# The last pass's first layer in two parts of three slices instead of three parts of two

## The chip, the cores and the metric

One core of a Trainium2 chip runs the whole program. The metric is the device time of one launch in microseconds (us), median over several runs. The engines are TensorE (PE in the profile; PEld is its weight load), VectorE (DVE), ScalarE (ACT), GpSimd (POOL) and the queue engine SyncE (SP). They run side by side[...].

## The reference

The input is an image batch x of 8 x 96 x 96 positions with 192 channels, in float32. Two residual blocks are applied one after the other. What follows is the reference cut to the second block's end, which is where the change lies:

```
x = x + L0(gn(x))            # group norm, 192->384, 3x3 conv, four scans, layer norm, 384->192
y = depthwise_conv7x7(gn(x)) + dw_bias
y = (y - mean(y)) * rsqrt(var(y) + 1e-6) * ln_gamma + ln_beta     # over the 192 channels
y = y @ w0 + b0              # 192 -> 768
y = gelu(y)
y = y @ w1 + b1              # 768 -> 192
x = x + y * gamma
```

## The kernel before

The program is five passes over the batch, one after the other, with arrays in device memory between them. The first pass normalizes, turns and projects x (lines 348 to 395). The second does the 3 x 3 convolution and the scans (L579 to L649). The third does the layer norm and the projection back to 192 channels (L831 to L865). The fourth does the 7 x 7 convolution, as products with band matrices (L1009, L1024), and leaves its result in `Y_d`. The last pass, from line 1093, does the rest of the second block: layer norm, first layer, gelu, second layer, residual. The change is in the last pass alone.

The last pass works in 96 units, `u` = 0 to 95. A unit is 768 positions: four image columns (`WH = 4`) of 96 rows for two images. Channels lie on partitions for the first layer, so the 192 channels of two images, 384 values, fill three blocks of 128 partitions, `yT[:, 0..2]`. Block 0 and block 2 hold 128 channels of one image each; block 1 holds the remaining 64 channels of one image in its upper half and of the other in its lower half.

The steps of a unit, each a function in the code:

- `stats_e(u, j)` and `norm_e(u, j)`, for j = 0 to 7: mean and variance of one column (L1144, L1145 on VectorE), the power -1/2 of the variance (L28 on VectorE, L29 on GpSimd), and the normalized values `yn` (L1154 on VectorE).
- `turn_in(u, k)`, k = 0 to 2: TensorE turns one block of `yn` by four transposes (L1169) into a PSUM tile `pt`, and VectorE copies it to `yT` (L1173).
- `first_layer(u, mb)`: the 768 outputs are NE = 6 slices of 128. For each slice m and image q there is one PSUM tile `hp` of 128 x 384. It takes one product with 128 channels on the contracted side (L1186) and one with 64 (L1196); then ScalarE applies the gelu and writes `g` (L1205).
- `second_layer(u, k)`, k = 0 to 2: one block of 128 positions of both images. For each image six products, one for each slice, are summed in a PSUM tile `po` (L1216). VectorE adds the residual `r` and writes `xo` (L1223), and GpSimd issues two transfers to the output (L1234).
- `load_r(u)`, `bias_r(u)`: the residual is loaded by SyncE's queue (L1124), and GpSimd adds the second layer's bias (L1133).

Every float32 product appears in the profile as two weight loads and two matmul records, a transpose as one of each. A first-layer part of two slices is therefore 8 records of L1186 and then 8 of L1196, and one `second_layer` call is 24 records of L1216. The two 64-channel products of a slice, for q = 0 and q = 1, use different halves of the partitions, and their records come in pairs that start within 0.01 us of each other.

The order on every engine is the order in which the code issues the instructions (`tc.manual_schedule()`). In the loop over units, three units are in work at once: the first layer of u, the second layer of u - 1, the turning of u + 1, and the statistics and normalization of u + 2. PSUM has eight banks for each partition. The pools of this pass take two for `pt`, four for `hp` and two for `po`. A pool hands out its banks in turn, and the first writer of a reused bank waits until the bank's last reader has finished:

```
ps_t = ph.enter_context(tc.tile_pool(name="e_ps_t", bufs=2, space=PSUM))
ps_h = ph.enter_context(tc.tile_pool(name="e_ps_h", bufs=4, space=PSUM))
ps_o = ph.enter_context(tc.tile_pool(name="e_ps_o", bufs=2, space=PSUM))
```

Of the kernel before, what the change touches and what calls it, by code (L numbers as in the profile page):

```python
# [8 lines left out]
F32 = mybir.dt.float32  # L9
# [3 lines left out]
PSUM = bass.MemoryType.PSUM  # L13
# [71 lines left out]
def conv_blocks_kernel(  # L85
# [32 lines left out]
    B, S, _, D = x.shape  # L118
# [4 lines left out]
    NE = EXP // 128  # L123
# [97 lines left out]
    with ExitStack() as ph:  # L221
# [6 lines left out]
        ps_t = ph.enter_context(tc.tile_pool(name="a_ps_t", bufs=2, space=PSUM))  # L228
# [239 lines left out]
        with tc.manual_schedule():  # L468
# [13 lines left out]
            for b in range(B):  # L482
                more = b + 1 < B
                for t in range(n_t):
                    u = b * n_t + t
# [279 lines left out]
    with ExitStack() as ph:  # L765
# [170 lines left out]
        n_u = BP * NH * n_c  # L936
# [153 lines left out]

    WH = 4
    WE = 2 * WH
    HE = 128 // WH
    with ExitStack() as ph:
        ip = ph.enter_context(tc.tile_pool(name="e_in", bufs=2))
        sp = ph.enter_context(tc.tile_pool(name="e_small", bufs=3))
        tp = ph.enter_context(tc.tile_pool(name="e_t", bufs=2))
        ps_t = ph.enter_context(tc.tile_pool(name="e_ps_t", bufs=2, space=PSUM))  # L1100
        ps_h = ph.enter_context(tc.tile_pool(name="e_ps_h", bufs=4, space=PSUM))
        ps_o = ph.enter_context(tc.tile_pool(name="e_ps_o", bufs=2, space=PSUM))

        def place(n):
            bp, n = divmod(n, PH * NV)
            return (bp, *divmod(n, NV))

        per = WQ // WH
        n_y = BP * PH * NV
        n_u = n_y * per  # L1110
        ys, rs_, mvs, rss, yns, yTs, gs, xos = {}, {}, {}, {}, {}, {}, {}, {}

        def load_y(n):
            bp, p, a = place(n)
            ys[n] = ip.tile([S, D, 2 * WQ], F32, tag="y", name=f"y_{n}")
            nc.sync.dma_start(ys[n], Y_d[PH - 1 - p :: PH, bp, a])

        def load_r(u):
            n, t = divmod(u, per)
            bp, p, a = place(n)  # L1120
            v = a * WQ + t * WH
            rs_[u] = ip.tile([128, S // HE, 2 * D], F32, tag="r", name="r", bufs=4)
            for k in range(S // HE):
                nc.sync.dma_start(  # L1124
                    rs_[u][:, k],
                    X2_d[bp, p, k * HE : (k + 1) * HE, v : v + WH].rearrange(
                        "h v b c -> h v (b c)"
                    ),
                )

        def bias_r(u):
            r = rs_[u].rearrange("p k (b c) -> p (k b) c", b=2)
            nc.gpsimd.tensor_tensor(  # L1133
                r, r, b1g.unsqueeze(1).to_broadcast([128, 2 * S // HE, D]), ALU.add
            )

        def stats_e(u, j):
            n, t = divmod(u, per)
            if j == 0:
                if t == 0 and n + 1 < n_y:  # L1140
                    load_y(n + 1)
                mvs[u] = sp.tile([S, WE, 2], F32, tag="mv", name="mv")
            st = sp.tile([S, 6], F32, tag="st", name="st", bufs=4)
            nc.vector.bn_stats(st, ys[n][:, :, t * WE + j])  # L1144
            nc.vector.bn_aggr(mvs[u][:, j], st)  # L1145
            if j == WE - 1:
                rss[u] = sp.tile([S, WE], F32, tag="rs", name="rs")
                rsqrt_eps(nc, sp, rss[u], mvs[u][:, :, 1], LN1_EPS, neg_half, "rs_ve")

        def norm_e(u, j):  # L1150
            n, t = divmod(u, per)
            if j == 0:
                yns[u] = sp.tile([S, WE, D], F32, tag="yn", name="yn", bufs=2)
            nc.vector.tensor_scalar(  # L1154
                yns[u][:, j],
                ys[n][:, :, t * WE + j],
                mvs[u][:, j, 0:1],
                rss[u][:, j : j + 1],
                ALU.subtract,
                ALU.mult,  # L1160
            )

        def turn_in(u, k):
            if k == 0:
                yTs[u] = tp.tile([128, 3, S, WH], F32, tag="yT", name="yT")
            yp = yns[u].rearrange("p (j i) c -> p j (i c)", i=2)
            pt = ps_t.tile([128, WH, S], F32, tag="pt", name="pt")
            for j in range(WH):
                nc.tensor.transpose(  # L1169
                    pt[:, j], yp[:, j, k * 128 : (k + 1) * 128], ident[:S, :S]  # L1170
                )

            nc.vector.tensor_copy(  # L1173
                yTs[u][:, k].rearrange("p h j -> p j h"), pt[:, :, ::-1]
            )

        def first_layer(u, mb):
            if mb == 0:
                gs[u] = tp.tile([128, NE, 2, WH * S], F32, tag="g", name="g")
            yT, g = yTs[u].rearrange("p k h j -> p k (h j)"), gs[u]  # L1180
            ms = (2 * mb, 2 * mb + 1)
            hps = {}
            for m in ms:
                for q in range(2):
                    hps[m, q] = ps_h.tile([128, WH * S], F32, tag="hp", name="hp")
                    nc.tensor.matmul(  # L1186
                        hps[m, q],
                        w0w[:, 2 * q, m * 128 : (m + 1) * 128],
                        yT[:, 2 * q],
                        start=True,  # L1190
                        stop=False,
                    )
            for m in ms:
                for q in range(2):
                    p = slice(q * DH, (q + 1) * DH)
                    nc.tensor.matmul(  # L1196
                        hps[m, q],
                        w0w[p, 1, m * 128 : (m + 1) * 128],
                        yT[p, 1],
                        start=False,  # L1200
                        stop=True,
                    )
            for m in ms:
                for q in range(2):
                    nc.scalar.activation(  # L1205
                        g[:, m, q], hps[m, q], AF.Gelu, bias=b0g[:, m : m + 1], scale=1.0
                    )

        def second_layer(u, k):
            if k == 0:  # L1210
                xos[u] = tp.tile([128, S // HE, 2, D], F32, tag="xo", name="xo")
            g, xo = gs[u], xos[u]
            po = ps_o.tile([128, 2, D], F32, tag="po", name="po")
            for q in range(2):
                for m in range(NE):
                    nc.tensor.matmul(  # L1216
                        po[:, q],
                        g[:, m, q, k * 128 : (k + 1) * 128],
                        w1g[:, m],
                        start=(m == 0),  # L1220
                        stop=(m == NE - 1),
                    )
            nc.vector.tensor_tensor(  # L1223
                xo[:, k].rearrange("p b c -> p (b c)"),
                po.rearrange("p b c -> p (b c)"),
                rs_[u][:, k],
                ALU.add,
            )
            n, t = divmod(u, per)
            bp, p, a = place(n)  # L1230
            w = (a * WQ + t * WH) * PH + p
            we = w + (WH - 1) * PH + 1
            for b in range(2):
                nc.gpsimd.dma_start(  # L1234
                    out[2 * bp + b, k * HE : (k + 1) * HE, w:we:PH, :], xo[:, k, b]
                )

        assert S // HE == 3
        with tc.manual_schedule():
            load_y(0)  # L1240
            load_r(0)
            for u in range(2):
                for j in range(WE):
                    stats_e(u, j)
                for j in range(WE):
                    norm_e(u, j)
                if u == 0:
                    for k in range(3):
                        turn_in(0, k)
            for u in range(n_u + 1):  # L1250
                for k in range(3):
                    if u < n_u:
                        first_layer(u, k)
                    if u + 1 < n_u:
                        turn_in(u + 1, k)
                    if k == 0:
                        if u + 1 < n_u:
                            load_r(u + 1)
                        if u < n_u:
                            bias_r(u)  # L1260
                    if u + 2 < n_u:
                        if k < 2:
                            for j in range(4 * k, 4 * k + 4):
                                stats_e(u + 2, j)
                        else:
                            for j in range(WE):
                                norm_e(u + 2, j)
                    if u >= 1:
                        second_layer(u - 1, k)


# [45 lines left out]
```

## Time and profile before

| what | value |
|---|---|
| time, three runs | 6007.35, 6009.42, 6020.1 us; median 6009.42 us |
| profiled execution | 6011.68 us; its span 6009.9 us |
| mean granted TensorE clock | 0.973 |
| PE busy | 5680.5 us, 95% of the span |
| PEld, DVE, ACT, POOL busy | 66%, 57%, 41%, 44% of the span |
| last pass on PE | from its first transpose at 3541.5 us to its last product near 5998 us |

The page gives busy shares over the whole span, but the five passes have different limits, so each pass has to be read by itself. In a group's row, the number after the last bar is the time in which the engine stood idle just before these instructions, and after the arrow stands what ended it. In the timeline, a row is a run of like instructions: its start, the time from the first one's start to the last one's end, the engine, the line, what is written and read, and how many. A matmul's modelled length is longer than its pitch, because matmuls overlap: the pitch is the distance of starts.

### The profile page before, as it was taken

How to read it: one execution, taken by the hardware profiler on the slowest of the kernel's cores; microseconds unless marked ns; L12 is line 12 of the kernel's file. 1: busy time of each engine (PE TensorE's matmuls, PEld its weight loads, DVE VectorE, ACT ScalarE, POOL GpSimd, SP SyncE). 2: the span in 40 equal slices, each digit the busy share in tenths (PEclk: the TensorE clock that was granted, in tenths of full speed). 3: DMA queues.
4: the chain of work that ended last, by engine and by line, in shares of the span. 5: the costliest groups of instructions: out<-in, count | busy, mean ns of one | idle time of the engine just before them, and what ended most of it. 6: DMA issues, size and time to landing. Idle time of an engine off the chain costs nothing.

```text
span 6009.9 us, 122810 instructions
## 1 busy us (share of the span) xinstructions
PE 5680.5 (95%) x48550; PEld 3943.4 (66%) x48550; DVE 3454.0 (57%) x8023; ACT 2440.3 (41%) x6146; POOL 2634.7 (44%) x2835
## 2 busy tenths in 40 slices
PE   6999989999998999999677769999999999999999
PEld 3655633333336989898666657777777777777777
DVE  5555469999995667777532334444444444444442
ACT  2444457777774555555333322222222222222221
POOL 1111148888886666666444422322332233233222
PEclk9999989999999999999888889999999999999999
DMA  7999779999987888888899952222222222222221
GB/s 206 282 285 258 219 213 243 244 242 244 244 231 210 266 261 268 262 267 261 232 286 290 284 141 69 66 72 63 79 64 78 64 79 64 78 64 77 61 64 37
DMA packets 570206, 1054.36 MB, mean 175 GB/s; under 512 B 109575, under 2 KB 426260, under 8 KB 567328
## 3 DMA queue, kind: packets, MB, share of 16 engines
q1 hardware_dynamic: 439344, 593.23, 37.8%
q0 software_dynamic: 124160, 450.67, 24.1%
q8 instruction: 384, 6.29, 0.5%
q10 hardware_dynamic: 6128, 2.61, 0.2%
q14 instruction: 190, 1.56, 0.1%
HBM read 585.19 MB, written 476.57 MB: 177 GB/s over the span
## 4 chain that ended last, share of the span: by engine, by line
PE 77%; DMA 6%; DVE 1%; issue 1%; SPq 1%; POOL 1%; ACT 0%; DVEq 0%; POOLq 0%; ACTq 0%
PE po L1216 19%; PE po L833 13%; PE hp L1186 12%; PE pl L579 10%; PE hp L1196 7%; PE pa L600 5%; PE pt L831 4%; DMA xin<-X_d 4%; PE py L1024 2%; PE pt L1169 2%; PE pa L603 2%; DMA Y_d<-yo 1%; DVE xin L1009 1%; DMA band<-Z_d 0%; SPq L1063 0%
## 5 line engine op out<-in xcount | busy, mean ns | idle before, releaser
L1205 ACT ACTIVATE g<-hp,b0g 128x384 f32<-128x384 f32 x1152 | 573.9, 580 | 1856.4 <-PE hp L1196 1856.4
L1216 PE MATMUL po<-w1g,g 128*128 128x192 f32 x6912 | 1178.3, 327 | 0.0
L1216 PEld LDWEIGHTS po<-w1g,g 128*128 128x128 f32 x6912 | 1116.6, 190 | 1.6 <-issue 1.1
L833 PE MATMUL po<-wc,mt 128*96 128x193 f32 x4608 | 912.8, 333 | 0.0
L1173 DVE COPY yT<-pt 128x384 f32<-128x384 f32 x288 | 251.4, 873 | 1126.7 <-PE pt L1169 1126.4
L1234 POOL DMA_DIRECT2D out_dram<-xo x576 | 321.3, 560 | 1147.9 <-DVE xo L1223 1119.4
L1186 PE MATMUL hp<-yT,w0w 128*128 128x384 f32 x2304 | 794.4, 488 | 0.4 <-ACT g L1205 0.4
L833 PEld LDWEIGHTS po<-wc,mt 128*96 128x96 f32 x4608 | 701.8, 163 | 68.6 <-ACT mean L837 65.0
L579 PE MATMUL pl<-pin,band 34*32 34x380 f32 (+1 forms) x13824 | 629.9, 489 | 19.3 <-DMA pin<-P_d 18.5
L1186 PEld LDWEIGHTS hp<-yT,w0w 128*128 128x128 f32 x2304 | 431.4, 191 | 231.6 <-issue 2.6
L609 DVE TENSOR_TENSOR_SCAN z<-decay,loc 128x768 f32<-128x768 f32 x288 | 505.9, 1756 | 61.2 <-ACT loc L588 31.7
L1024 PE MATMUL py<-xin,band 63*64 63x248 f32 (+1 forms) x6912 | 405.5, 394 | 138.3 <-DVE xin L1009 136.2
L649 POOL TENSOR_TENSOR mo<-mo,z 128x768 f32<-128x768 f32 x288 | 529.6, 1839 | 3.3 <-ACT mo L604 0.4
L618 DVE TENSOR_TENSOR_SCAN z<-decay,z 128x768 f32<-128x768 f32 x288 | 498.2, 1730 | 0.0
L579 PEld LDWEIGHTS pl<-pin,band 34*32 34x32 f32 x13824 | 232.8, 107 | 398.7 <-issue 397.1
L1024 PEld LDWEIGHTS py<-xin,band 63*64 63x64 f32 x6912 | 345.0, 142 | 198.5 <-DVE xin L1009 123.5
L840 ACT ACTIVATE sq<-pt,mean 96x384 f32<-96x384 f32 x768 | 443.0, 577 | 25.7 <-ACT mean L837 0.8
L1196 PE MATMUL hp<-yT,w0w 64*128 64x384 f32 x2304 | 449.4, 508 | 0.0
L600 PE MATMUL pa<-loc,mix 128*32 128x384 f32 x3456 | 431.9, 493 | 0.0
L603 PE MATMUL pa<-last,down 96*32 96x384 f32 x1152 | 426.9, 493 | 0.9 <-ACT mo L604 0.9
L29 POOL TENSOR_TENSOR rs<-rs_ve,neg_half 96x8 f32<-96x8 f32 x96 | 158.6, 1652 | 606.3 <-DVE rs_ve L28 606.3
L362 PE MATMUL pm<-xT,win 128*128 128x384 f32 x1152 | 395.9, 494 | 3.3 <-DVE po L386 3.3
(116 smaller groups left out, 7707.4 us busy)
## 6 DMA issues: line engine op xcount, KB each, us to landing
P_d<-po POOLq DMA_DIRECT2D x96, 1152.0 KB, 9.9
pin<-P_d SPq DMA_DIRECT2D x192, 576.0 KB
mt<-M_d SPq DMA_DIRECT2D x576, 192.0 KB
xq<-in_x_dram SPq DMA_DIRECT2D x96, 576.0 KB
xr<-in_x_dram SPq DMA_DIRECT2D x384, 144.0 KB
X_d<-x1u POOLq DMA_DIRECT2D x192, 288.0 KB, 4.2
X_d<-x1c SPq DMA_DIRECT2D x192, 288.0 KB
y<-Y_d SPq DMA_DIRECT2D x24, 2304.0 KB
```

What stands on the lines that cost most here:

```text
L579: nc.tensor.matmul(pls[g][at * RB : (at + 1) * RB, :, lo:hi], band[rows, c, kh, :], pin[rows, c, :, NJ - 1 - j, lo + kh - 1 : hi + kh - 1] ...
L600: nc.tensor.matmul(pa[at], mix[:, i, at], loc[:, q], start=True, stop=True)
L603: nc.tensor.matmul(pa[at], down[:, to], last[:, q], start=True, stop=True)
L609: nc.vector.tensor_tensor_scan(zf, decay_f, loc.rearrange("p q n -> p (q n)"), 0.0, ALU.mult, ALU.add)
L618: nc.vector.tensor_tensor_scan(zr, decay_f, zr, 0.0, ALU.mult, ALU.add)
L649: nc.gpsimd.tensor_tensor(m, m, z, ALU.add)
L833: nc.tensor.matmul(po[:S, b], lhs[m], wc[:, m], start=(m == 0), stop=(m == NC - 1))
L1024: nc.tensor.matmul(pys[t // 2][g][k * 64 : (k + 1) * 64, t % 2, :, lo:hi], pair[k][0][rows, c, d * ZS : d * ZS + 64], pair[k][1][rows, t, ...
L1186: nc.tensor.matmul(hps[m, q], w0w[:, 2 * q, m * 128 : (m + 1) * 128], yT[:, 2 * q], start=True, stop=False,)
L1196: nc.tensor.matmul(hps[m, q], w0w[p, 1, m * 128 : (m + 1) * 128], yT[p, 1], start=False, stop=True,)
L1205: nc.scalar.activation(g[:, m, q], hps[m, q], AF.Gelu, bias=b0g[:, m : m + 1], scale=1.0)
L1216: nc.tensor.matmul(po[:, q], g[:, m, q, k * 128 : (k + 1) * 128], w1g[:, m], start=(m == 0), stop=(m == NE - 1),)
```

## The change

The first layer of a unit is issued in two parts of three slices, where it was three parts of two. A part needs six `hp` tiles at once, so the PSUM pools are divided anew: one bank for `pt`, and seven in one pool that `hp` and `po` share. The loop body over k is written out, since the parts no longer go one with each k. On TensorE, a unit's order was

first layer (2 slices), turn 0, second layer 0; first layer (2), turn 1, second layer 1; first layer (2), turn 2, second layer 2

and becomes

first layer (3 slices), turn 0, second layer 0, turn 1; first layer (3), turn 2, second layer 1, second layer 2.

On VectorE the copies of turn 1 and turn 2 now follow one another, the second half of the statistics comes after both, and the normalization stands between the residual additions of second layer 1 and second layer 2. The orders on ScalarE, GpSimd and the SyncE queue stay as they were.

```diff
-        ps_t = ph.enter_context(tc.tile_pool(name="e_ps_t", bufs=2, space=PSUM))
-        ps_h = ph.enter_context(tc.tile_pool(name="e_ps_h", bufs=4, space=PSUM))
-        ps_o = ph.enter_context(tc.tile_pool(name="e_ps_o", bufs=2, space=PSUM))
+        ps_t = ph.enter_context(tc.tile_pool(name="e_ps_t", bufs=1, space=PSUM))
+        ps_h = ph.enter_context(tc.tile_pool(name="e_ps_h", bufs=7, space=PSUM))
...
-            ms = (2 * mb, 2 * mb + 1)
+            ms = range(mb * NE // 2, (mb + 1) * NE // 2)
...
-            po = ps_o.tile([128, 2, D], F32, tag="po", name="po")
+            po = ps_h.tile([128, 2, D], F32, tag="hp", name="po")
...
-                for k in range(3):
-                    if u < n_u:
-                        first_layer(u, k)
-                    if u + 1 < n_u:
-                        turn_in(u + 1, k)
-                    if k == 0:
-                        if u + 1 < n_u:
-                            load_r(u + 1)
-                        if u < n_u:
-                            bias_r(u)
-                    if u + 2 < n_u:
-                        if k < 2:
-                            for j in range(4 * k, 4 * k + 4):
-                                stats_e(u + 2, j)
-                        else:
-                            for j in range(WE):
-                                norm_e(u + 2, j)
-                    if u >= 1:
-                        second_layer(u - 1, k)
+                if u < n_u:
+                    first_layer(u, 0)
+                if u + 1 < n_u:
+                    turn_in(u + 1, 0)
+                    load_r(u + 1)
+                if u < n_u:
+                    bias_r(u)
+                if u + 2 < n_u:
+                    for j in range(4):
+                        stats_e(u + 2, j)
+                if u >= 1:
+                    second_layer(u - 1, 0)
+                if u + 1 < n_u:
+                    turn_in(u + 1, 1)
+                if u < n_u:
+                    first_layer(u, 1)
+                if u + 1 < n_u:
+                    turn_in(u + 1, 2)
+                if u + 2 < n_u:
+                    for j in range(4, WE):
+                        stats_e(u + 2, j)
+                if u >= 1:
+                    second_layer(u - 1, 1)
+                if u + 2 < n_u:
+                    for j in range(WE):
+                        norm_e(u + 2, j)
+                if u >= 1:
+                    second_layer(u - 1, 2)
```

## The prediction

> **What bounds the kernel now.** I read the page first: PE is busy 95% of the span. A share over five passes decides nothing, so I asked for the last pass alone, by stretches (columns: window, its length, then busy us with record counts for PE, PEld, DVE, ACT and POOL, clock, DMA share, GB/s), and for its PE groups between 4000 and 5900 us.
>
> ```profile
> 3700.00:4500.00 800.00, 800.00 (x4155) 597.50 (x4154) 365.69 (x972) 188.96 (x380) 239.07 (x251) 1.00 0.26 71
> 5300.00:5960.00 660.00, 660.00 (x3426) 492.89 (x3425) 296.28 (x782) 155.44 (x312) 195.85 (x207) 1.00 0.23 64
> ```
>
> ```profile
> L1216 PE MATMUL po<-w1g,g 128*128 128x192 f32 x5381 | 917.7, 327 | 0.0
> L1186 PE MATMUL hp<-yT,w0w 128*128 128x384 f32 x1792 | 614.5, 486 | 0.0
> L1196 PE MATMUL hp<-yT,w0w 64*128 64x384 f32 x1792 | 349.6, 508 | 0.0
> L1169 PE MATMUL pt<-ident,yn 96*128 96x96 f32 x896 | 123.0, 260 | 0.0
> ```
>
> PE is busy in every microsecond at full clock; no group shows idle time ahead of it; DVE, the next, is busy 46% (365.69 of 800). TensorE alone sets this pass, and it waits for nobody. So fewer waits cannot be the gain. What can shrink is the time that the stream itself takes, and for that I read the starts in the timeline of one third of a unit, up to the next third's start.
>
> ```profile
> 5003.54 2.74 PE L1186 MATMUL hp<-yT,w0w 128*128 128x384 f32 x8
> 5006.21 1.56 PE L1196 MATMUL hp<-yT,w0w 64*128 64x384 f32 x8
> 5007.71 0.55 PE L1169 MATMUL pt<-ident,yn 96*128 96x96 f32 x4
> 5008.09 4.09 PE L1216 MATMUL po<-w1g,g 128*128 128x192 f32 x24
> 5012.02 2.74 PE L1186 MATMUL hp<-yT,w0w 128*128 128x384 f32 x8
> ```
>
> A third takes 8.48 us (5012.02 - 5003.54), a unit 25.44. Pitch of a record is (length of the run - one record) / (number - 1). L1186: (2.74 - 0.486) / 7 = 0.322. For the others the first pass helps, where the same shapes stand in other neighbourhoods:
>
> ```profile
> 299.67 1.14 PE L375 MATMUL pm<-xT,win 64*128 64x384 f32 x6
> 300.74 0.55 PE L348 MATMUL pt<-ident,xq 96*128 96x96 f32 x4
> 301.12 4.06 PE L362 MATMUL pm<-xT,win 128*128 128x384 f32 x12
> 305.02 0.82 PE L348 MATMUL pt<-ident,xq 96*128 96x96 f32 x8
> 305.78 2.21 PE L375 MATMUL pm<-xT,win 64*128 64x384 f32 x12
> ```
>
> L375 x12 is six 64-row pairs, L1196 x8 is four; two pairs more cost 2.21 - 1.56 = 0.65, so a pair has a pitch of 0.325 (0.322 from single starts). Transposes after a 128-row product (L348 x8): (0.82 - 0.246) / 7 = 0.082. After 64-row pairs (L348 x4): (0.55 - 0.246) / 3 = 0.101, so 0.055 more in the three pitches together. L1216 has 0.1625 by single starts in the trace.
>
> At those pitches a third is 8 x 0.3225 + 4 x 0.3225 + 4 x 0.0825 + 24 x 0.1625 = 8.10 us. The other 0.38 us lies where one kind gives way to another:
>
> - last L1186 to first L1196: it starts at 5006.28 - 0.486 = 5005.80, the pair at 5006.21, so 0.416 for 0.3225: 0.094.
> - first pair to second: (1.56 - 0.482) - 2 x 0.3225 = 0.43 for 0.3225: 0.105.
> - last pair to first transpose: 5007.71 - (5007.77 - 0.482) = 0.42, and 0.413 by the single starts from the pair's second member, for 0.316: 0.097.
> - first transpose to second: 0.055, as above.
> - after transposes, the first 128-row product to the second: 0.030 (L362 x12: 4.06 - 0.486 - 11 x 0.322 = 0.03; L1216 shows the same).
>
> The sum is 0.381, which closes the third. The first four, 0.351 us, are the price of one visit to the 64-row products.
>
> **What the Trainium skill says.** TensorEngine Tiling (Array Packing), Tiling Modes, Key Properties: a change of tiling mode, as from 128 rows to two 64-row tiles, drains TensorE. It gives no price; the trace agrees, with 0.094 going in and 0.097 coming out beside the re-filling costs. TensorE: Matmul & The Clock Gate, Part 1, "Wait — 56ns, not 53.3ns?": a warm start-to-start of N / 2.4 GHz + 2.5 ns. With N taken as twice the columns it gives 322.5, 162.5 and 82.5 ns for the three shapes, my pitches, so the steady stream has no slack left. Same page, same part, "What's actually happening": after an idle window of some 3.4 us the clock halves until TensorE is busy again. The trace agrees: after 40.64 us of idleness the first L1186 run, at 3545.86, takes 5.37 us for the later 2.74. PSUM — Partial Sum Buffer, Specifications: 8 banks; the new split, 1 + 7, uses all.
>
> **The change part by part.**
>
> 1. Products, transposes, weight loads, gelus, transfers: none is removed or added. The data each touches is the same.
>
> 2. First layer in two parts: three visits to 64-row products become two. A visit's price does not grow with its pairs: L375's visits have six pairs, as the new parts will, and by the figures above still only one long pitch. A unit saves 0.351 us.
>
> 3. Turn 1 no longer follows 64-row pairs but second layer 0. The first pass has that seam: from the last L362, at 301.12 + 4.06 - 0.486 = 304.69, to the first L348 of eight, at 305.02, is 0.33, the plain pitch of L362; by single starts the next transpose is 0.005 late. Turn 1 then precedes L1186, and pays the 0.030 that it used to pay ahead of L1216. Three such seams before, three after. Cost: 0.005 per unit.
>
> 4. Second layer 1 and 2 back to back: L1216 after L1216, the plain pitch. Nothing.
>
> New unit: 24.30 + 2 x 0.351 + 3 x 0.030 + 0.005 = 25.10 us, against 24.30 + 3 x 0.381 = 25.44. **Saved: 0.345 us.**
>
> 5. Waits that the smaller pools add. I laid the new unit out at these pitches: first layer part one 0 to 6.10, turn 0 to 6.49, second layer 0 to 10.42, turn 1 to 10.75, part two to 16.9, turn 2 to 17.3, second layers 1 and 2 to 21.2 and 25.1. The other engines' durations:
>
> ```profile
> 5007.16 1.99 ACT L1205 ACTIVATE g<-hp,b0g 128x384 f32<-128x384 f32 x4 [6.43 <-PE hp L1196]
> 5016.77 0.86 DVE L1173 COPY yT<-pt 128x384 f32<-128x384 f32 x1 [3.99 <-PE pt L1169]
> 5017.48 3.07 DVE L1154 TENSOR_SCALAR yn<-y,mv,rs 96x192 f32<-96x192 f32 x8
> 5020.70 0.56 DVE L1223 TENSOR_TENSOR xo<-po,r 128x384 f32<-128x384 f32 x1 [0.16 <-PE po L1216]
> ```
>
> - Seven shared banks, in turn: `hp` 0 to 5, `po` 6, `hp` 7 to 12, `po` 13, `po` 14. Part two needs the banks of part one. ScalarE starts 0.95 us after the first 64-row product and takes 0.5 each, so it has freed all six at 7.9; part two begins at 10.75. Behind a late one would stand all of part two on TensorE. `po` 14 takes a bank whose gelu ends at about 16.3, and is wanted at 21.2. Part one of the next unit needs the bank of second layer 1, freed at 22.0, wanted at 28.
> - One `pt` bank: turn 1 (10.42) waits for the copy of turn 0, done at 7.6; turn 2 (16.9) for the copy of turn 1, done at 12.1 because the addition of second layer 0 stands ahead of it. This is the narrowest: 2.8 us. Behind turn 1 stands part two.
> - VectorE, late in the unit: four statistics (0.59 each) to 20.9, the addition of second layer 1 to 22.0; the power on GpSimd (1.65 us, plus signals) holds the normalization to about 23.4; it ends at 26.5, the addition of second layer 2 at 27.1. Next to need it: turn 0 at 31.2. Output issues wait for that addition and nobody on TensorE for them.
> - The transfers keep their order on the SyncE and POOL queues. At 26% DMA share and with residuals loaded a unit ahead, a shift of a few us is hidden.
>
> So waits cost nothing, with 2.8 us to spare per unit. Bounds: 0 and, if all is lost again, 0.345 per unit. I take 0.
>
> 6. Ends. Units 1 to 94 save 94 x 0.345 = 32.4. Unit 95, without turns, saves about 0.3. In unit 0 the normalization of unit 2 holds TensorE (3.5 us of idleness at 3552, 0.45 at 3574); VectorE's order there changes, and one part of the first layer more is done before it: I reckon between 2 gained and 1 lost, and take 0.5 gained.
>
> Sum: 32.4 + 0.3 + 0.5 = 33 us. From the profiled span, 6009.9, that gives 5977; its run took 6011.68, inside the three runs, so from the median 6009.42: **5976 us**.
>
> **The rivals.** What a measurement can tell from no change is about 0.2%, 12 us.
>
> A, the forecast: TensorE sheds 96 visits to the 64-row products, 30 to 37 us. For it: busy without a gap, and the seams priced in two passes. Chance 0.84.
>
> B, part of it is lost: the new seams at turn 1 drain too, or the clock halves once more in the ramp. Half saved is 16.5 us, 5993. Against it: L362 and L348 meet without loss. Chance 0.09.
>
> C, no change: the price belongs to the pairs rather than to the visit, so with 12 pairs in either order nothing is saved: 6009. Against it: L375's six pairs. Or the pools' waits eat it. Chance 0.03.
>
> D, slower: the single `pt` bank. If the copy of turn 0 came late on VectorE, turn 1 and all of part two would wait, every unit. It decides when the copy is more than 2.8 us late, and outweighs the saving beyond 2.8 + 0.345 = 3.15. Even the four statistics ahead of the copy (2.6 us) would not do it; the 3.07 us of normalization and the 0.56 of an addition together would: 3.63 - 3.15 = 0.5 a unit, 46 us, 6055. Against it: VectorE is done at 27.1 and turn 0 ends at 31.5. Chance 0.04.
>
> **How the numbers follow.** A's own range is 5970 to 5983: 96 x 0.38 = 36.5 and 2 in the ramp at the low end. The runs before reach 11 us above their median, so 5976 + 11 = 5987; taking in most of B, 5967 to 5991. Faster by over 0.2%: A and B, 0.93. Within: 0.03. Slower: 0.04.
>
> **What would show it.** Right: L1196 runs of 12, of about 2.2 us; a unit of 25.1 us; no idle time ahead of PE groups; turn 0 with 0.55, turn 1 with 0.50 for its four. Wrong: a unit near 25.4 with PE unbroken (C), or PE idle ahead of L1169 released by the copy L1173 or of L1186 by L1205 (D).

## The result and the profile after

| | before | changed |
|---|---|---|
| median, four runs each | 6012.9 us | 5985.45 us |
| lowest to highest | 6007.35 to 6020.1 us | 5978.23 to 5989.78 us |
| profiled span | 6009.9 us | 5988.0 us |
| mean granted clock | 0.973 | 0.973 |

The ratio is 0.9952, with a 95% interval of 0.9935 to 0.997: the change saves 0.5%, between 18 and 39 us. The forecast was 5976 us with a range of 5967 to 5991.

The stretches of the changed kernel's last pass (columns as before: window, length, then busy us with record counts of PE, PEld, DVE, ACT, POOL, clock, DMA share, GB/s), and its PE groups between 4000 and 5900 us:

```profile
3700.00:4500.00 800.00, 800.00 (x4206) 612.80 (x4207) 373.16 (x992) 185.69 (x380) 251.02 (x256) 1.00 0.26 72
5300.00:5940.00 640.00, 640.00 (x3372) 490.59 (x3371) 291.37 (x769) 149.91 (x306) 197.82 (x203) 1.00 0.23 65
```

```profile
L1216 PE MATMUL po<-w1g,g 128*128 128x192 f32 x5469 | 918.0, 327 | 0.0
L1186 PE MATMUL hp<-yT,w0w 128*128 128x384 f32 x1812 | 611.2, 487 | 0.0
L1196 PE MATMUL hp<-yT,w0w 64*128 64x384 f32 x1812 | 333.0, 500 | 0.0
L1169 PE MATMUL pt<-ident,yn 96*128 96x96 f32 x908 | 120.8, 255 | 0.0
```

TensorE is as busy as it was, and waits as little. Yet the same 800 us hold 4206 records where there were 4155. That is why a busy share could not have shown the gain: the lost time between kinds of product counts as busy, because records overlap. One unit in the timeline, up to its last second layer:

```profile
5011.83 4.03 PE L1186 MATMUL hp<-yT,w0w 128*128 128x384 f32 x12
5015.79 2.21 PE L1196 MATMUL hp<-yT,w0w 64*128 64x384 f32 x12
5017.93 0.55 PE L1169 MATMUL pt<-ident,yn 96*128 96x96 f32 x4
5018.31 4.09 PE L1216 MATMUL po<-w1g,g 128*128 128x192 f32 x24
5022.24 0.50 PE L1169 MATMUL pt<-ident,yn 96*128 96x96 f32 x4
5022.58 4.06 PE L1186 MATMUL hp<-yT,w0w 128*128 128x384 f32 x12
5026.57 2.21 PE L1196 MATMUL hp<-yT,w0w 64*128 64x384 f32 x12
5028.71 0.55 PE L1169 MATMUL pt<-ident,yn 96*128 96x96 f32 x4
5029.09 7.99 PE L1216 MATMUL po<-w1g,g 128*128 128x192 f32 x48
```

The runs of L1196 have twelve records and take 2.21 us; turn 0 and turn 2 take 0.55, turn 1 takes 0.50. L1186 takes 4.06 after transposes and 4.03 after products, which is the 0.030. From the 10th to the 90th unit the trace gives 25.093 us per unit, against 25.440 before: 0.347 saved.

The whole saving is smaller than 96 times that. Measured from the last pass's first transpose, whose time varies with the passes ahead of it, the last product starts after 2456.3 us before and after 2429.8 us now, 26.5 less. From unit 2 on, 32.7 us are saved (2401.96 against 2369.31). The first two units lose 6.2: unit 2 begins 60.50 us after the first transpose, where it was 54.34. These are parts of the beginning of the last pass on PE, first before and then changed, each down to the first product of unit 2; in brackets stands the idle time before a run and what ended it.

```profile
3541.53 0.39 PE L1169 MATMUL pt<-ident,yn 96*128 96x96 f32 x1 [40.64 <-DVE yn L1154]
...
3545.00 0.90 PE L1169 MATMUL pt<-ident,yn 96*128 96x96 f32 x4 [0.28 <-DVE yT L1173]
...
3556.22 0.28 PE L1169 MATMUL pt<-ident,yn 96*128 96x96 f32 x1 [3.50 <-DVE yn L1154]
...
3595.86 2.74 PE L1186 MATMUL hp<-yT,w0w 128*128 128x384 f32 x8
```

```profile
3546.11 0.39 PE L1169 MATMUL pt<-ident,yn 96*128 96x96 f32 x1 [41.72 <-DVE yn L1154]
...
3549.58 0.90 PE L1169 MATMUL pt<-ident,yn 96*128 96x96 f32 x4 [0.92 <-DVE yT L1173]
3551.40 0.90 PE L1169 MATMUL pt<-ident,yn 96*128 96x96 f32 x4 [0.92 <-DVE yT L1173]
3552.26 5.62 PE L1186 MATMUL hp<-yT,w0w 128*128 128x384 f32 x12
3557.80 2.21 PE L1196 MATMUL hp<-yT,w0w 64*128 64x384 f32 x12
3562.62 0.39 PE L1169 MATMUL pt<-ident,yn 96*128 96x96 f32 x1 [2.61 <-DVE yn L1154]
...
3566.10 0.90 PE L1169 MATMUL pt<-ident,yn 96*128 96x96 f32 x4 [0.93 <-DVE yT L1173]
3566.79 6.84 PE L1186 MATMUL hp<-yT,w0w 128*128 128x384 f32 x12
...
3606.61 4.03 PE L1186 MATMUL hp<-yT,w0w 128*128 128x384 f32 x12
```

With one `pt` bank the transposes wait for a copy, 0.92 and 0.93 us each; with two, the one such wait ahead of the loop was 0.28. And L1186 x12 takes 6.84 us instead of 4.03: apart from the first 9 us, in which both kernels have half the clock, the granted clock was halved here from 3562.1 to 3572.4 and from 3586.0 to 3589.4; before, only from 3557.8 to 3561.2. The gaps between TensorE's records in the beginning add up to 10.15 us, where they were 6.75; its work there takes 50.35 us, where it was 47.59, though it has two visits fewer.

### The profile page after: what moved, and what is told of

Same layout as the page of the kernel before. It is cut to its first block, busy times and chain, and to the rows that moved or that the text cites. A ratio compares the mean times of both kernels' runs of the same rounds, so it can differ in the third digit from the quotient of the medians.

```text
span 5988.0 us, 122717 instructions
## 1 busy us (share of the span) xinstructions
PE 5651.6 (94%) x48550; PEld 3956.6 (66%) x48550; DVE 3455.9 (58%) x8023; ACT 2432.1 (41%) x6146; POOL 2659.4 (44%) x2835
## 3 DMA queue, kind: packets, MB, share of 16 engines
q14 instruction: 191, 1.56, 0.1%
## 4 chain that ended last, share of the span: by engine, by line
PE 77%; DMA 6%; DVE 1%; issue 1%; POOL 1%; SPq 1%; ACT 0%; DVEq 0%; POOLq 0%; ACTq 0%
PE po L1216 19%; PE po L833 13%; PE hp L1186 12%; PE pl L579 10%; PE hp L1196 7%; PE pa L600 5%; PE pt L831 4%; DMA xin<-X_d 3%; PE py L1024 2%; PE pa L603 2%; PE pt L1169 2%; DMA Y_d<-yo 2%; DVE xin L1009 1%; DMA band<-Z_d 0%; SPq L1063 0%
## 5 line engine op out<-in xcount | busy, mean ns | idle before, releaser
L1216 PE MATMUL po<-w1g,g 128*128 128x192 f32 x6912 | 1161.4, 327 | 0.0
L1216 PEld LDWEIGHTS po<-w1g,g 128*128 128x128 f32 x6912 | 1120.3, 190 | 1.1 <-issue 1.1
L1186 PE MATMUL hp<-yT,w0w 128*128 128x384 f32 x2304 | 781.8, 489 | 0.4 <-DVE yT L1173 0.4
L1234 POOL DMA_DIRECT2D out_dram<-xo x576 | 344.4, 600 | 876.1 <-DVE xo L1223 848.9
L1186 PEld LDWEIGHTS hp<-yT,w0w 128*128 128x128 f32 x2304 | 429.7, 191 | 257.5 <-issue 3.6
L1196 PE MATMUL hp<-yT,w0w 64*128 64x384 f32 x2304 | 423.5, 500 | 0.0
```

Source lines behind the costliest of these rows:

```text
L1186: nc.tensor.matmul(hps[m, q], w0w[:, 2 * q, m * 128 : (m + 1) * 128], yT[:, 2 * q], start=True, stop=False,)
L1196: nc.tensor.matmul(hps[m, q], w0w[p, 1, m * 128 : (m + 1) * 128], yT[p, 1], start=False, stop=True,)
L1216: nc.tensor.matmul(po[:, q], g[:, m, q, k * 128 : (k + 1) * 128], w1g[:, m], start=(m == 0), stop=(m == NE - 1),)
```

## The experiments

Unit lengths below are means over the 10th to the 90th unit, from the trace. "Beginning" is the time from the last pass's first transpose to the first product of unit 2.

**Pools alone.** The kernel before with the changed pools:

```diff
-        ps_t = ph.enter_context(tc.tile_pool(name="e_ps_t", bufs=2, space=PSUM))
-        ps_h = ph.enter_context(tc.tile_pool(name="e_ps_h", bufs=4, space=PSUM))
-        ps_o = ph.enter_context(tc.tile_pool(name="e_ps_o", bufs=2, space=PSUM))
+        ps_t = ph.enter_context(tc.tile_pool(name="e_ps_t", bufs=1, space=PSUM))
+        ps_h = ph.enter_context(tc.tile_pool(name="e_ps_h", bufs=7, space=PSUM))
...
-            po = ps_o.tile([128, 2, D], F32, tag="po", name="po")
+            po = ps_h.tile([128, 2, D], F32, tag="hp", name="po")
```

> The kernel before, with its loop and its two-slice parts, but with the changed kernel's PSUM pools: one bank for pt, seven shared by hp and po. Theory (the gain is the price of visits to the 64-row products, the ramp's loss comes from the single pt bank and from GpSimd's bias addition): three visits per unit stay, so the steady unit stays 25.44 us with no idle time ahead of PE groups; the three turns of unit 0 ahead of the loop take about 1.8 us longer, since each waits for the copy of the one before. Whole kernel: 1 to 4 us over the kernel before, within the noise. Rival (the shared pools change the steady state): a unit other than 25.44 us.

Measured: 6014.5 against 6013.45 us, ratio 1.0003 (0.9994 to 1.0012). The unit is 25.440 us, as before. The turns ahead of the loop take 6.13 us from the first transpose to the first product instead of 4.33, and the beginning 57.30 instead of 54.34. The pools cost about 3 us once and nothing per unit; the gain is not theirs.

**Four visits.** The changed kernel, each part in two halves:

```diff
-            for m in ms:
-                for q in range(2):
-                    hps[m, q] = ps_h.tile([128, WH * S], F32, tag="hp", name="hp")
...
+            for some in (ms[:2], ms[2:]):
+                for m in some:
+                    for q in range(2):
+                        hps[m, q] = ps_h.tile([128, WH * S], F32, tag="hp", name="hp")
...
+                for m in some:
+                    for q in range(2):
+                        p = slice(q * DH, (q + 1) * DH)
```

> The changed kernel in its order and pools, but each part of three slices goes to the 64-row products twice, after two slices and after the third: four visits per unit instead of two. Theory (price per visit): two more visits, each 0.094 going in, 0.105 at the first pair, 0.097 coming out and about 0.105 at the second record of L1186 after it, 0.40 us: the unit grows from 25.10 to about 25.90 us, the kernel by about 77 us over the changed one, some 45 us over the kernel before. Rival (the order, second layers side by side and turn 1 elsewhere, made the gain): the unit stays near 25.1 us.

Measured, in one run: 6060.24 us, 47 above the kernel before (6013.45); unit 25.888 us. One part in its timeline, where L1187 and L1197 stand for L1186 and L1196:

```profile
5011.45 2.77 PE L1187 MATMUL hp<-yT,w0w 128*128 128x384 f32 x8
5014.15 1.56 PE L1197 MATMUL hp<-yT,w0w 64*128 64x384 f32 x8
5015.64 1.56 PE L1187 MATMUL hp<-yT,w0w 128*128 128x384 f32 x4
5017.13 0.92 PE L1197 MATMUL hp<-yT,w0w 64*128 64x384 f32 x4
```

The third run shows the price of coming back: four records at the plain pitch would take 0.486 + 3 x 0.3225 = 1.45 us, these take 1.56. The order of turns and second layers is the changed kernel's, and the unit is longer than the one before the change: the order is not what gains.

**Six visits.** The kernel before, the 64-row products after each slice:

```diff
                     )
-            for m in ms:
                 for q in range(2):
                     p = slice(q * DH, (q + 1) * DH)
```

> The kernel before with its order and pools, but in each part the 64-row products follow each slice: six visits per unit instead of three. Theory: 25.44 + 3 x 0.40 = 26.64 us per unit, about 115 us over the kernel before. Rival (the price belongs to the pairs, of which there are as many): 25.44 us, no change.

Measured, in one run: 6125.48 us, 112 above the kernel before; unit 26.633 us. One part in its timeline, where L1195 stands for L1196:

```profile
5009.06 1.45 PE L1186 MATMUL hp<-yT,w0w 128*128 128x384 f32 x4
5010.44 0.92 PE L1195 MATMUL hp<-yT,w0w 64*128 64x384 f32 x4
5011.29 1.56 PE L1186 MATMUL hp<-yT,w0w 128*128 128x384 f32 x4
5012.78 0.92 PE L1195 MATMUL hp<-yT,w0w 64*128 64x384 f32 x4
```

With two, three, four and six visits, units are 25.09, 25.44, 25.89 and 26.63 us, where the visits added in the last two return to L1186 and cost 0.40 each. A unit has the same twelve pairs in all four; only the number of visits differs.

**No 64-row products.** The changed kernel with all sums over block 1 taken over its 128 rows, so that the first layer mixes the two images' channels:

```diff
-                    p = slice(q * DH, (q + 1) * DH)
                     nc.tensor.matmul(
                         hps[m, q],
-                        w0w[p, 1, m * 128 : (m + 1) * 128],
-                        yT[p, 1],
+                        w0w[:, 1, m * 128 : (m + 1) * 128],
+                        yT[:, 1],
```

> The changed kernel, but the 64-row products are done over all 128 rows of the block, so the sums mix the two images' channels (the output is not the reference's): no change of tiling mode is left in the unit, and 24 full records take the place of 12 pairs. Theory (the price is the change of tiling mode): L1196 follows L1186 and L1169 follows L1196 at the plain pitch of 0.3225, the second transpose starts 0.087 after the first; the unit is 24.30 + 12 x 0.3225 + 3 x 0.035 = 28.27 us. Rival (the price is a change of line, of shape or of operands): 0.35 more per visit, 28.97 us.

Measured, in one run: 6287.95 us; unit 28.263 us. In its timeline, L1195 stands for L1196:

```profile
5020.06 4.03 PE L1186 MATMUL hp<-yT,w0w 128*128 128x384 f32 x12
5023.93 4.03 PE L1195 MATMUL hp<-yT,w0w 128*128 128x384 f32 x12
5027.80 0.49 PE L1169 MATMUL pt<-ident,yn 96*128 96x96 f32 x4
```

From L1186 to L1195 is 12 x 0.3225 = 3.87 us exactly, and turn 0 takes 0.49 instead of 0.55. Neither the change of line nor of operands costs anything; the change between 128-row products and 64-row pairs does. Since this kernel drops the 64 rows and the pairing together, it does not tell which of the two makes the price. The pairs are worth their price all the same: doing without them costs 28.26 - 25.09 = 3.17 us per unit.

**The beginning.** The next four kernels were timed five times each on one chip, the kernel before at 6013.52 us (median of nine). First the changed kernel once more.

> The changed kernel once more, on the chip of the three versions that follow. Theory: 94 steady units save 0.345 us each, unit 95 saves 0.2, the ramp of units 0 and 1 loses 6.2 of it: 26 us under the kernel before, ratio 0.9957. If the ramp's loss in the first profile was chance, the saving is nearer 33 us, 0.9945.

Measured: 5986.6 us, ratio 0.9952 (0.9939 to 0.9965). The beginning took 60.04 us in its profile: the loss was not chance. The clock's part in it varied: halved for 6.8 and 3.4 us, where the first profile had 10.3 and 3.4.

Then two banks for `pt`:

```diff
-        ps_t = ph.enter_context(tc.tile_pool(name="e_ps_t", bufs=1, space=PSUM))
-        ps_h = ph.enter_context(tc.tile_pool(name="e_ps_h", bufs=7, space=PSUM))
+        ps_t = ph.enter_context(tc.tile_pool(name="e_ps_t", bufs=2, space=PSUM))
+        ps_h = ph.enter_context(tc.tile_pool(name="e_ps_h", bufs=6, space=PSUM))
```

> The changed kernel with two banks for pt and six shared by hp and po. Theory (the single pt bank lengthened the ramp): the turns of unit 0 take 4.3 us from the first transpose to the first product instead of 6.15, and turn 1 of unit 1 no longer waits 0.93 us for a copy: 2 to 4 us under the changed kernel; the steady unit stays 25.10 us, since the narrowest of the bank waits still has about 1 us to spare. Rival (the ramp's loss is GpSimd's bias addition beside the normalization, or chance): 0 to 1 us. If six shared banks are too few, PE shows idle time ahead of L1186 or L1216 released by L1205 or L1223, and the gain is lost.

Measured: 5982.95 us, ratio 0.9946 (0.9932 to 0.9959). Its interval overlaps the changed kernel's, so the gain is read from the trace: 4.31 us to the first product, beginning 54.92 us, 5.1 to 5.6 less than with one bank and more than the 2 to 4 expected. The unit stays 25.093: six shared banks are enough.

Then, on top of that, the bias addition moved:

```diff
             load_r(0)
+            bias_r(0)
...
-                if u < n_u:
-                    bias_r(u)
...
                 if u >= 1:
                     second_layer(u - 1, 2)
+                if 1 <= u < n_u:
+                    bias_r(u)
```

> The kernel with two pt banks, and GpSimd's bias addition (L1133) moved: for unit 0 ahead of the first statistics, for the others to the end of the loop body. Theory (in the ramp the bias addition runs beside the normalization of units 1 and 2 and makes it 5.3 us long instead of 3.05): both normalizations take 3.05 us, the ramp is 3 to 5 us shorter than with two pt banks alone; the steady unit stays 25.10. Rival (the long normalization has another cause): it stays at 5.3 us and the time does not change.

Measured: 5977.02 us, ratio 0.9937 (0.9924 to 0.9949); beginning 48.43 us, 6.5 less than with two banks alone (3 to 5 were expected), unit 25.093. First the normalization of unit 1 and GpSimd's work beside it in the changed kernel, then in this one:

```profile
3559.75 5.32 DVE L1154 TENSOR_SCALAR yn<-y,mv,rs 96x192 f32<-96x192 f32 x8 [1.75 <-POOL rs L29]
3559.67 2.62 POOL L1133 TENSOR_TENSOR r<-r,b1g 128x1152 f32<-128x1152 f32 x1
```

```profile
3558.93 3.08 DVE L1154 TENSOR_SCALAR yn<-y,mv,rs 96x192 f32<-96x192 f32 x8 [1.75 <-POOL rs L29]
3541.77 2.62 POOL L1133 TENSOR_TENSOR r<-r,b1g 128x1152 f32<-128x1152 f32 x1 [22.02 <-DMA r<-X_d]
```

Beside the addition the normalization is 2.24 us longer, nearly the addition's 2.62: that is what VectorE would lose if it stood still for it. The Trainium skill, SBUF — State Buffer, Who interferes with whom, says that the two engines share one pair of ports under an exclusive lock, that some VectorE instructions need it, `tensor_scalar` in certain modes among them, and that the loser blocks. The single records agree: the addition starts 0.08 us ahead, the first of the eight normalizations takes 2.73 us, and the other seven take 0.43 to 0.46. Statistics (L1144) beside the same addition, in the kernel with the bias moved, keep their 0.44 to 0.46, so it does not hold up every instruction of VectorE. Whether the normalization ran in one of those modes, no run here shows.

The same holds for unit 2's (5.32 and 3.12 us). The kernel before has this collision as well:

```profile
3553.35 5.32 DVE L1154 TENSOR_SCALAR yn<-y,mv,rs 96x192 f32<-96x192 f32 x8 [1.75 <-POOL rs L29]
3569.96 5.19 DVE L1154 TENSOR_SCALAR yn<-y,mv,rs 96x192 f32<-96x192 f32 x8
```

So what the moved bias saves is a further gain, and no part of what the change lost. It is more than twice 2.24: of the 6.5, TensorE's gaps are 3.6 us shorter and its work 2.9; the granted clock is not halved again after 3554.2, where with two banks alone it was from 3557.3 to 3564.1.

**Turns together.** On top of that, turn 1 behind turn 0:

```diff
                 if u + 1 < n_u:
                     turn_in(u + 1, 0)
+                    turn_in(u + 1, 1)
                     load_r(u + 1)
...
-                if u + 1 < n_u:
-                    turn_in(u + 1, 1)
                 if u < n_u:
                     first_layer(u, 1)
```

> The kernel with two pt banks and the bias moved, and turn 1 issued right after turn 0, both behind the first part's 64-row products. Theory (every change from transposes to 128-row products costs 0.030, every change into transposes after 128-row products 0.005): a unit has one such seam fewer, 25.06 us, 3.4 us less over 96 units. Rival (the two turns together make TensorE wait for a pt bank or VectorE): idle time ahead of L1169, and no gain.

Measured: 5972.87 us, ratio 0.9927 (0.9915 to 0.994), 13.7 us under the changed kernel on the same chip. Its interval overlaps the former kernel's, so the unit decides: 25.060 us, 0.033 less, with no idle time ahead of any PE group.

```profile
5021.81 0.88 PE L1169 MATMUL pt<-ident,yn 96*128 96x96 f32 x8
5022.52 4.09 PE L1216 MATMUL po<-w1g,g 128*128 128x192 f32 x24
5026.45 4.03 PE L1186 MATMUL hp<-yT,w0w 128*128 128x384 f32 x12
```

**Products right behind the pairs.** The kernel with the bias moved, with no turn behind 64-row products:

```diff
                 if u + 1 < n_u:
-                    turn_in(u + 1, 0)
                     load_r(u + 1)
...
                 if u >= 1:
                     second_layer(u - 1, 0)
                 if u + 1 < n_u:
+                    turn_in(u + 1, 0)
                     turn_in(u + 1, 1)
                 if u < n_u:
                     first_layer(u, 1)
-                if u + 1 < n_u:
-                    turn_in(u + 1, 2)
...
                 if u >= 1:
                     second_layer(u - 1, 1)
+                if u + 1 < n_u:
+                    turn_in(u + 1, 2)
```

> The kernel with two pt banks and the bias moved, but no turn stands behind 64-row products: turns 0 and 1 follow second layer 0, turn 2 follows second layer 1, so L1216 follows L1196 directly. Theory (the second weight load after a change of mode is exposed, 0.055 for a 96-row transpose and, by the three such places at the end of the first profile, 0.105 for L1216): a unit is 24.30 + 2 x (0.094 + 0.105 + 0.097 + 0.105) + 2 x 0.035 = 25.17 us, 0.08 more than with turns behind the pairs. Rival (the 0.055 belongs to the transposes, and is avoided by moving them): 25.02 us.

Measured, in one run: 5977.24 us; unit 25.159 us, 0.066 more than 25.093.

```profile
5011.63 2.21 PE L1196 MATMUL hp<-yT,w0w 64*128 64x384 f32 x12
5013.77 4.17 PE L1216 MATMUL po<-w1g,g 128*128 128x192 f32 x24
5017.77 0.49 PE L1169 MATMUL pt<-ident,yn 96*128 96x96 f32 x4
5018.10 4.09 PE L1216 MATMUL po<-w1g,g 128*128 128x192 f32 x24
```

L1216 x24 takes 4.17 us behind pairs, 4.09 behind transposes, and would take 4.06 behind its own kind (0.326 + 23 x 0.1625). In these runs the second record after the pairs is late whatever it is, by 0.105 for L1186 and L1216 and by 0.055 for a transpose: the turns stood in a good place. Twice the difference of 0.05, less the 0.030 of one change out of transposes that falls away, comes to 0.07, near the 0.066 measured.

## Why the prediction was right

**Steps 1 and 2, the visits: right in kind and size.** Forecast 0.345 us per unit, measured 0.347. Four, six and no visits gave 25.888, 26.633 and 28.263 us where 25.90, 26.64 and 28.27 were expected. The price is one of changing between 128-row products and 64-row pairs; it does not grow with the pairs (rival C) and does not lie in the order.

**Steps 3 and 4, the seam at turn 1 and the second layers back to back: right.** 0.50 us for the four transposes of turn 1, 0.030 at the L1186 that follows. The 48 records of L1216 take 0.326 + 47 x 0.1625 + 0.030 = 7.99 us, the plain pitch but for the change from transposes.

**Step 5, the waits in the steady state: right.** No PE group waits. The layout of VectorE's work also held; here is the late part of the unit that begins at 5011.83:

```profile
5033.22 0.56 DVE L1223 TENSOR_TENSOR xo<-po,r 128x384 f32<-128x384 f32 x1 [0.57 <-PE po L1216]
5034.49 3.10 DVE L1154 TENSOR_SCALAR yn<-y,mv,rs 96x192 f32<-96x192 f32 x8 [0.71 <-POOL rs L29]
5037.51 0.54 DVE L1223 TENSOR_TENSOR xo<-po,r 128x384 f32<-128x384 f32 x1
5043.61 0.90 DVE L1173 COPY yT<-pt 128x384 f32<-128x384 f32 x1 [5.56 <-PE pt L1169]
```

The normalization ends 25.8 us into the unit (forecast 26.5), the last addition 26.2 (27.1), and VectorE then stands idle for 5.56 us before the copy of turn 0: rival D had that much room and more.

**Step 6, the beginning: mis-sized.** I reckoned 0.5 us gained, between 2 gained and 1 lost. With unit 1's 0.345 the beginning was to be 0.8 shorter; it is 6.2 us longer, a miss of 7.0. The waits for the one `pt` bank, which step 5 priced at nothing in the steady state, were never laid out for the units in which VectorE is behind. Two banks took 5.6 of the 7.0 back: TensorE's gaps in the beginning went from 10.15 us to 7.59, and its work from 50.35 to 47.33. The first part is waiting; the second goes with the halved clock that rival B named for the ramp, 6.8 us of it instead of 13.7. How much of that the waits themselves brought on stays open, since the repeat of the changed kernel, with the same waits, had 10.2 us of it.

Step 6 also misread a wait. The 3.50 us of idleness that ends at 3556.22 before is a wait for the normalization of unit 1 (the one at 3553.35, issued ahead of the loop), which the change does not move; only the 0.45 at 3574 is unit 2's. Nor was the idle window of some 3.4 us, which the prediction quotes, needed for a halved clock: in the changed kernel TensorE's work ended at 3560.01, and the clock was halved from 3562.1 on, after 2.1 us.

The rest of the distance to the forecast is not the change's: the median of before moved from 6009.42 to 6012.9 with a fourth run. Less the 26.5 us by which the last pass is shorter, that gives 5986.4; 5985.45 was measured. That the two agree within 1 us is luck, since whole runs of either kernel spread over more than 11. The time lies inside the stated range, but above A's own 5970 to 5983: it is the 11 us allowed for the spread of runs that hold it.

## What to carry to other kernels

When an engine is busy without a gap and waits for nobody, look at the starts of its records where one kind gives way to another: what is lost there is counted as busy, and is removed by grouping like with like as far as the buffers allow. Lay out a new order not only in the steady state but also for the first units, where a helper engine is still behind and a saved buffer does bind. Read a gain of a fraction of a per cent from the length of a unit in the trace, since here it repeats to a few ns while whole runs differ by 10 us and more.

## What the runs showed of the hardware

- Beyond the plain pitch, a visit from 128-row products to 64-row pairs cost TensorE 0.094 us going in, 0.105 from the first pair to the second, 0.097 coming out, and once more at the second record after: 0.055 where transposes followed, 0.105 where 128-row products followed. It was the same for visits of two, four and six pairs.
- Eight normalizations of 96 x 192 on VectorE took 3.05 us alone and 5.32 us beside a GpSimd addition of 2.62 us; the first of them took 2.73 us and bore the whole loss.
- The granted clock was halved after 2.1 us without TensorE work in the changed kernel (3560.01 to 3562.1, by the modelled end of its last record), and after 2.2 us in the one with two banks (3555.12 to 3557.3).
- The start of the last pass wandered from 3538.4 to 3550.5 us among eleven profiles, though their first four passes are the same. So the passes ahead bring a spread of up to 12 us into whole times, in which the last pass has no part.
